# A conditional arm moved behind the ending of a two-layer hybrid kernel, and routing lists built for 60 units in place of 86

## The chip, the cores and the metric

The kernel runs on one core of a Trainium2 chip. The metric is the device time of one execution in microseconds (us). The core has five engines with a queue each: PE (TensorE, with weight loads shown as PEld), DVE (VectorE), ACT (ScalarE), POOL (GpSimd) and SP (SyncE, which here only issues transfers and loads registers). Each engine works through its own instructions in order and waits on semaphores for the others.

## The reference

The input is an image of 256 channels by 64 by 64. Layer 0 is a windowed linear attention and is not touched by the change. Layer 1 works on 4096 tokens of 256 channels: full softmax attention, then a mixture of eight experts of which each token uses two. What matters here is the expert part:

```python
logits = xt @ Wr + br
probs = jax.nn.softmax(logits, axis=-1)
top_p, top_idx = jax.lax.top_k(probs, TOP_K)          # TOP_K = 2 of 8 experts
weights = top_p / top_p.sum(axis=-1, keepdims=True)
...
h = jax.nn.gelu(jnp.einsum('end,edh->enh', xe, W1) + b1[:, None, :], approximate=False)
y = jnp.einsum('enh,ehd->end', h, W2) + b2[:, None, :]
...
out = (weights[:, :, None] * sel).sum(axis=1)         # added to t, then back to channels x pixels
```

## The kernel before

**Slots and units.** The kernel doesn't run every expert on every token. It gathers tokens by expert into units of 128 rows; two units make a slot of 256 rows, and some slots have a third unit of 64 rows. Four early slots (EARLY) are filled from the first tiles while attention still runs. The other 28 usual slots (NS) take 60 units (`USUAL = THIRDS + 2 * NS`). In the worst case the tokens of an input need up to 86 units (NU). Whether the 26 beyond the usual ones are needed is known only at run time.

**Lists.** `route_and_run` ranks the router's logits, counts tokens per expert, and gives every token a place: a unit (`which`) and a row in it (`within`). From these it builds, for each of the 86 units, the list of the token rows to read (`source`) and of the rows to write (`target`). It does this with one-hot matrices in eight steps of eight token tiles. In each step DVE builds `line` (L1690) and two thirds of `piece` (L1693 and L1697), ACT the other third (L1696), and PE adds eight small products into the PSUM tile `back` (L1699, shown as ps_acc). A piece is 8 x NU elements wide per partition. A helper `owners` (L1628 to L1650) works out which expert each slot belongs to, for the usual slots and the 26 later units alike, and the flag `more_slots`. At the end `row_ops` (L972 to L978) turns `back` into `source` and `target`. PE's matmuls for the early slots go on between these products.

**The slots themselves.** `run` is a generator over slots. For each slot SP loads the weights of the expert (L1380; for usual slots it first loads the expert's number into a register, L1360), POOL gathers the rows (L1401, from the DRAM tensor `zrows`), PE transposes them (L1420), PE and ACT compute the hidden layer (L1450 matmul, L1453 gelu), PE the second product (L1467), DVE adds the bias (L1471), and POOL scatters the rows to the DRAM tensor `yrows` (L1472). `zrows` is written by SP (L1525) from rows that ACT scales (L1521) between the gelus of the early slots. The order of all these on each engine is set by a scheduler, which follows the order of the program text but moves instructions by its own estimate of their times.

**The arm and the ending.** All of the attention and of the usual slots stands in the taken side of a branch (`tc.If(tame > 0)`, L1744). Behind it every engine loads the flag `more_slots` into a register (L2028) and branches on it (L2030, `tc.If(more > 0)`). The arm computes units 60 to 85. When it is skipped, each engine jumps over it to a short block that brings the semaphores to the values that the arm would have left, and from there to the ending. In that short block POOL waits for all its scatters and then raises the semaphores of its own transfers (INC_SWDGE_SEM). Then comes the ending: for four bands of the image and two groups of four tiles in each, SP loads the rows of the first expert and ACT those of the second from `yrows` (L2048, 512 KB each, four buffers per set), DVE adds both into the residual `t` with the router's weights `top` (L2052, two instructions a tile), PE transposes (L2058), ACT copies to the image (L2059), and SP and ACT store one band at a time (L2065). The last lines, L2090, are the waits and barriers that end the program.

Of the kernel before, what the change touches and what calls it, by code (L numbers as in the profile page):

```python
# [56 lines left out]
AWAY = 200.0 * P  # L57
TAME = 60.0
# [62 lines left out]
def tile_conv_attn_hybrid(ctx: ExitStack, tc: tile.TileContext, a: dict, out: bass.AP):  # L121
# [100 lines left out]
    def tok(i):  # L222
        return slice(P * i, P * (i + 1))
# [757 lines left out]
    def all_of(ops):  # L981
        for op in ops:
            op()
# [169 lines left out]
    with ExitStack() as phase:  # L1153
# [196 lines left out]
        more_slots = of_last(1, dt=I32)  # L1350

# [134 lines left out]

        def route_and_run(work_on, slot_ps, beside, done):

            with ExitStack() as experts:
# [16 lines left out]
                with ExitStack() as routing:  # L1506
# [73 lines left out]
                    size, ends, begins = (small.tile([P, 2, NE], F32, name=x) for x in ("size", "ends", "begins"))  # L1580
# [15 lines left out]
                    units_used = small.tile([P, 1], F32, name="units_used")  # L1596
# [26 lines left out]
                    def owners():  # L1623

                        n = NU - USUAL
                        slot_of = small.tile([P, NS + n], F32, name="slot_of")
                        late, unit = slot_of[:, NS:], cst["unit"]
                        over = small.tile([P, n], F32, name="over")  # L1628
                        full = small.tile([P, 1], F32, name="full")
                        nc.vector.tensor_copy(slot_of[:, :NS], iota[:, :NS])  # L1630
                        nc.vector.tensor_scalar_add(full, units_used, float(THIRDS))
                        nc.vector.tensor_scalar(over, unit[:, :n], full, None, op0=ALU.is_ge)
                        nc.vector.scalar_tensor_tensor(
                            late, unit[:, 2 * n :], units_used, over, op0=ALU.subtract, op1=ALU.mult
                        )
                        nc.vector.tensor_add(late, late, unit[:, n : 2 * n])
                        past = small.tile([P, NS + n, 2 * NE], F32, name="past")
                        nc.vector.tensor_tensor(
                            past,
                            slot_of.unsqueeze(2).to_broadcast([P, NS + n, 2 * NE]),  # L1640
                            ends.rearrange("p n e -> p (n e)").unsqueeze(1).to_broadcast([P, NS + n, 2 * NE]),
                            ALU.is_ge,
                        )
                        owner = small.tile([P, NS + n], F32, name="owner")
                        nc.vector.tensor_reduce(owner, past, AX.X, ALU.add)
                        nc.vector.tensor_copy(expert_of, owner)
                        nc.vector.tensor_single_scalar(expert_of, expert_of, NE - 1, op=ALU.bitwise_and)
                        nc.vector.tensor_scalar_add(full, with_thirds, float(NS - THIRDS))
                        nc.vector.tensor_tensor(full, full, slots_used, ALU.max)
                        nc.vector.tensor_single_scalar(more_slots, full, float(NS), op=ALU.is_gt)  # L1650
# [22 lines left out]
                    NPC = NU  # L1673
                    G = 8
                    counter = r_work.tile([P, P, G], BF16, name="counter", bufs=1)
                    nc.gpsimd.tensor_copy(counter, iota.unsqueeze(2).to_broadcast([P, P, G]))
                    units = r_work.tile([P, NPC], BF16, name="units", bufs=1)
                    nc.gpsimd.tensor_copy(units, iota[:, :NPC])
                    back = r_ps.tile([P, CH], F32, tag="acc", name="ps_acc", bufs=1)
                    for n in range(2):  # L1680
                        pos = one(f"pos{n}")
                        whole, low = (small.tile([P, NT], I32, name=f"{x}{n}") for x in ("whole", "part"))
                        which, within = (small.tile([P, NT], BF16, name=f"{x}{n}") for x in ("which", "within"))
                        all_of(position_ops(hots[n], row, each(f"at{n}"), pos, whole, low, within, which, 0))
                        high = small.tile([P, NT], BF16, name=f"high{n}")
                        nc.gpsimd.tensor_copy(high, cst["high"][:, NT * n : NT * (n + 1)])
                        for i8 in range(0, NT, G):
                            some = lambda v, n: v[:, i8 : i8 + G].unsqueeze(1).to_broadcast([P, n, G])
                            line = r_work.tile([P, P, G], BF16, name="line")
                            made = nc.vector.tensor_tensor(line, some(within, P), counter, ALU.is_equal)  # L1690
                            piece = r_work.tile([P, 3, G, NPC], BF16, name="piece")
                            on_units = lambda v: v[:, i8 : i8 + G].unsqueeze(2).to_broadcast([P, G, NPC])
                            nc.vector.tensor_tensor(  # L1693
                                piece[:, 0], on_units(which), units.unsqueeze(1).to_broadcast([P, G, NPC]), ALU.is_equal
                            )
                            nc.scalar.activation(piece[:, 1], piece[:, 0], AF.Copy, scale=cst["number"])  # L1696
                            nc.vector.tensor_mul(piece[:, 2], piece[:, 0], on_units(high))  # L1697
                            for i in range(G):
                                nc.tensor.matmul(  # L1699
                                    back[:, : 2 * NPC].rearrange("p (m n) -> p m n", m=2),  # L1700
                                    line[:, :, i],
                                    piece[:, 1:, i, :],
                                    start=n == 0 and i8 + i == 0,
                                    stop=n == 1 and i8 + i == NT - 1,
                                )
                            if n == 0 and i8 == G:
                                with tc.issue_after(made.ins):
                                    owners()
                            advance(1)

                    advance(2)
# [3 lines left out]
                    high = small.tile([P, NPC], F32, name="high")  # L1715
                    nc.vector.tensor_copy(high, back[:, NPC : 2 * NPC])
                    got, second, spare = (small.tile([P, NPC], F32, name=x) for x in ("got", "second", "spare"))
                    all_of(row_ops(source, target, back[:, :NPC], high, got, second, spare, cst["spare"]))
# [309 lines left out]
        more = nc.values_load(more_slots[:1, :1], min_val=0, max_val=1)  # L2028
        with (
            tc.If(more > 0),  # L2030
            psum("m_ps2", 2) as ps,
        ):
            one_bank = lambda: ps.tile([P, KC * SLOT], F32, tag="tp", name="ps_tp")
            for _ in run([(None, q) for q in range(USUAL, NU)], [ps], [], {}, one_bank):
                pass

        with ExitStack() as ending:
            pool = lambda name, bufs: ending.enter_context(tc.tile_pool(name=name, bufs=bufs))
            ps = ending.enter_context(psum("o_ps", 4))
            work = pool("o_work", 4)  # L2040
            img = act.rearrange("p k (y x) -> p k y x", x=IMG)
            by_band = yrows[: 2 * N, :].rearrange("(n i b p) c -> n b p i c", n=2, b=NB, p=P)
            for b in range(NB):
                for i4 in range(0, NCH, 4):
                    ys = []
                    for n in range(2):
                        ys.append(work.tile([P, 4, C], F32, tag=f"y{n}", name=f"y{n}"))
                        (nc.scalar if n else nc.sync).dma_start(ys[n], by_band[n, b, :, i4 : i4 + 4, :])  # L2048
                    for i in range(4):
                        at = NB * (i4 + i) + b  # L2050
                        for n in range(2):
                            nc.vector.scalar_tensor_tensor(  # L2052
                                t[:, at, :C], ys[n][:, i, :], top[n][:, at : at + 1], t[:, at, :C],
                                op0=ALU.mult, op1=ALU.add,
                            )
                        op = ps.tile([P, CH], F32, tag="mm", name="ps_mm")
                        for k in range(KC):
                            nc.tensor.transpose(op[:, tok(k)], t[:, at, tok(k)], ident)  # L2058
# [35 lines left out]
```

## Time and profile before

| | us |
|---|---|
| median of 3 runs | 2750.59 (2749.43 to 2750.81) |
| the profiled execution | 2754.69 |
| its span in the trace | 2752.9 |
| busy PE / DVE / ACT / POOL | 2638.8 / 1880.4 / 1502.6 / 820.5 |
| lists are built (first line to last product) | 2240.0 to 2262.7 |
| last expert matmuls end | about 2704.5 |
| last scatter to `yrows` issued | 2705.24 |
| first load of the ending issued | 2713.44 |
| last store of the ending issued | 2747.7 |

Times inside the execution are microseconds from the start of the span. A row of a group gives a line of the kernel, an engine, an operation and its tile, then how often it ran, its shortest, median and longest time in ns, and when the first and the last of them began. "POOLq", "SPq" and the like are the sequencers of the engines: instructions that only wait, branch, load registers or issue a transfer.

### The profile page before, as it was taken

What the parts mean: (1) busy time and instruction counts of PE and PEld (TensorE: products, weight loads), DVE (VectorE), ACT (ScalarE), POOL (GpSimd) and SP (SyncE); (2) the same over time, 40 slices, a digit from 0 to 9 for tenths busy, and PEclk for the clock granted to TensorE, in tenths of its full rate; (3) what the DMA queues carried; (4) which work ended last, traced back from release to release, by engine and by line L of the source; (5) the groups of instructions that cost most, each with busy time, mean ns of one, the idle gap of its engine ahead of it and who ended that gap; (6) DMA issues with size and microseconds to landing.
All of it is one profiled execution on the core that took longest, in us unless ns stands there. A gap on an engine that the chain in (4) does not pass through costs nothing.

```text
span 2752.9 us, 71916 instructions
## 1 busy us (share of the span) xinstructions
PE 2638.8 (96%) x30978; PEld 1189.6 (43%) x30978; DVE 1880.4 (68%) x2534; ACT 1502.6 (55%) x2079; POOL 820.5 (30%) x919
## 2 busy tenths in 40 slices
PE   6889999997999999999999999999999999999995
PEld 5454336744433556211212121212121278888883
DVE  6758688666878876788888888888888871111114
ACT  3323323222333334899898989898989852222222
POOL 2057777404777752000000010000001123222220
PEclk9999999999999999999999999999999999999996
DMA  5000000000000000455555555555656645555555
GB/s 145 7 23 25 11 28 22 7 13 23 21 15 25 25 22 1 91 118 115 113 113 113 119 112 108 116 116 110 139 107 137 153 147 175 194 187 179 187 174 193
DMA packets 114467, 256.65 MB, mean 93 GB/s; under 512 B 19890, under 2 KB 76440, under 8 KB 100052
## 3 DMA queue, kind: packets, MB, share of 16 engines
q0 software_dynamic: 22240, 132.66, 23.1%
q1 hardware_dynamic: 84724, 110.30, 12.4%
q10 hardware_dynamic: 7168, 8.92, 1.0%
q8 instruction: 247, 4.05, 0.6%
q14 instruction: 88, 0.72, 0.1%
HBM read 118.64 MB, written 17.86 MB: 50 GB/s over the span
## 4 chain that ended last, share of the span: by engine, by line
PE 91%; DVE 3%; DMA 3%; issue 2%; ACT 0%; POOL 0%; ACTq 0%; SPq 0%; DVEq 0%; POOLq 0%
PE ps_three L1799 19%; PE ps_acc L1758 18%; PE ps_sc L826 8%; PE ps_yp L1467 7%; PE ps_hp L1450 7%; PE ps_acc L842 7%; PE ps_sc L726 3%; PE ps_sc L753 3%; PE ps_acc L784 3%; PE ps_two L411 2%; PE ps_mm L1242 2%; PE ps_two L444 2%; DMA yrows<-v,qk 2%; PE ps_two L525 1%; PE ps_acc L772 1%
## 5 line engine op out<-in xcount | busy, mean ns | idle before, releaser
L1799 PE MATMUL ps_three<-qk 32*64 32x512 f32 x6144 | 563.2, 612 | 2.3 <-DVE t L1737 1.3
L1799 PE MATMUL ps_one<-qk 32*64 32x512 f32 x2048 | 556.2, 613 | 0.2 <-ACT pe L1808 0.2
L646 ACT COPY sm<-ps_sc 128x384 f32<-128x384 f32 (+3 forms) x454 | 218.3, 510 | 526.5 <-PE ps_sc L826 339.0
L1831 DVE TENSOR_TENSOR act<-act,pe 128x2048 f32<-128x2048 f32 x195 | 448.1, 2298 | 83.4 <-ACT pe L1811 51.3
L1811 ACT ACTIVATE pe<-ps_three 128x1536 f32<-128x1536 f32 x330 | 477.4, 1447 | 0.0
L653 DVE TENSOR_TENSOR sm<-ps_sc,mask 128x512 f32<-128x512 f32 (+3 forms) x740 | 340.1, 519 | 69.2 <-PE ps_sc L826 66.1
L653 POOL TENSOR_TENSOR sm<-sm,mask 128x192 f32<-128x192 f32 (+3 forms) x428 | 349.5, 846 | 114.3 <-ACT sm L646 114.0
L1831 DVE TENSOR_TENSOR act<-act 128x2048 f32<-128x2048 f32 x150 | 343.8, 2292 | 50.3 <-ACT act L1811 37.1
L1819 POOL DMA_DIRECT2D pe<-pe x108 | 93.0, 861 | 940.1 <-ACT pe L1811 625.1
L1758 PE MATMUL ps_acc<-pe,v 128*32 128x512 f32 x2640 | 351.6, 605 | 0.0
L1453 ACT ACTIVATE v<-ps_hp,qk 128x256 f32<-128x256 f32 (+1 forms) x256 | 122.8, 480 | 342.8 <-PE ps_hp L1450 338.5
L1799 PEld LDWEIGHTS ps_three<-qk 32*64 32x64 f32 x6144 | 112.5, 129 | 414.5 <-ACT pe L1808 243.2
L1811 ACT ACTIVATE act<-ps_three 128x1536 f32<-128x1536 f32 x182 | 263.2, 1446 | 0.0
L1467 PE MATMUL ps_yp<-qk,v 128*128 128x256 f32 (+1 forms) x1088 | 241.7, 380 | 0.0
L1450 PE MATMUL ps_hp<-qk 128*128 128x256 f32 (+1 forms) x1024 | 236.8, 389 | 2.8 <-ACT v L1453 1.7
L826 PE MATMUL ps_sc<-qk 32*64 32x384 f32 (+3 forms) x3584 | 234.6, 458 | 0.1
L1808 ACT ACTIVATE pe<-ps_one 128x512 f32<-128x512 f32 x330 | 197.3, 598 | 59.0 <-PE ps_one L1799 34.5
L653 POOL TENSOR_TENSOR sm<-sm,ycut 128x384 f32<-128x384 f32 (+4 forms) x146 | 147.1, 1028 | 254.1 <-ACT sm L646 253.8
L1467 PEld LDWEIGHTS ps_yp<-qk,v 128*128 128x128 f32 (+1 forms) x1088 | 200.3, 187 | 30.7 <-issue 1.3
L842 PE MATMUL ps_acc<-sm,v 128*32 128x256 f32 (+3 forms) x2688 | 213.2, 419 | 0.1
L1450 PEld LDWEIGHTS ps_hp<-qk 128*128 128x128 f32 x1024 | 180.7, 189 | 52.7 <-ACT v L1453 13.6
L1758 PE MATMUL ps_acc<-act,v 128*32 128x512 f32 x1456 | 193.9, 604 | 0.0
(359 smaller groups left out, 2868.7 us busy)
## 6 DMA issues: line engine op xcount, KB each, us to landing
pe<-pe POOLq DMA_DIRECT2D x108, 1024.0 KB
qk<-in_L_ffn_W SPq DMA_DIRECT2D x64, 1024.0 KB
by<-recs SPq DMA_DIRECT2D x48, 256.0 KB
rows<-in_x SPq DMA_DIRECT2D x16, 256.0 KB
qk<-in_L_ffn_b SPq DMA_DIRECT2D x32, 128.0 KB
y<-yrows SPq DMA_DIRECT2D x8, 512.0 KB
y<-yrows ACTq DMA_DIRECT2D x8, 512.0 KB
rec<-recs SPq DMA_DIRECT2D x60, 64.0 KB
```

Of the source, the lines that this page charges most:

```text
L646: copied = nc.scalar.copy(sm[:, :used], sc[:, :used])
L653: done = engine.tensor_mul(to, of, mk.unsqueeze(1).to_broadcast(list(to.shape)))
L826: nc.tensor.matmul(scs[h][u : u + rows, at : at + n], kT[hs[h], P * i + u : P * i + u + rows], qT[hs[h], CH * ix + CELL * c0 : CH * ix + C ...
L842: nc.tensor.matmul(acc[hs[h], CELL * c0 : CELL * c1], v[:, i, hs[h]], sms[h][:, at : at + n], start=not begun[0], stop=last and at == plac ...
L1450: nc.tensor.matmul(hp[:, :n], w1[:, k, tok(m)], x_now[:, k, :n], start=k == 0, stop=k == KC - 1)
L1453: done["gelu"] = nc.scalar.activation(hid[:, m, :n], hp[:, :n], AF.Gelu, bias=cols[:, m : m + 1]).ins
L1467: product = nc.tensor.matmul(yp[:n], hid[:, m, P * j : P * j + n], w2[:, m, :], start=m == 0, stop=m == NH - 1)
L1758: nc.tensor.matmul(to[D * hd : D * (hd + 1), :], lhsT(hd), rhs(hd), start=start, stop=stop, skip_group_check=True,)
L1799: nc.tensor.matmul(to[CELL * u : CELL * (u + 1), :], qk[hs, 1, g, P * i + CELL * u : P * i + CELL * (u + 1)], qk[hs, 0, g, chunk(qc)], sta ...
L1808: first = nc.scalar.activation(head(pe, 0), one, AF.Exp, scale=C**-0.5)
L1811: nc.scalar.activation(pe[:, CH:], three.rearrange("p h n -> p (h n)"), AF.Exp, scale=C**-0.5).ins
L1831: latest[:] = [nc.vector.tensor_add(total, total, weights_of[r, i]).ins]
```

## The change

Three things are done. First, the ending becomes a function `finish_all` that is called unconditionally straight behind the attention branch; the flag is loaded and tested after it, and the arm, if taken, computes the extra units and then calls `finish_all` once more. So that it can be called twice, the ending no longer adds into `t`: the first instruction of a tile writes into the first loaded buffer and the second into the second loaded buffer, which PE then transposes. Second, the code that builds the lists becomes `lists_of(first, last, ...)`. The usual path calls it for units 0 to 59; a piece is now 8 x 60 elements. The arm calls it again for units 60 to 85. Third, `owners_of` does the owners of one range: 28 slots on the usual path, the 26 later units in the arm. What the arm needs later (`ends`, `units_used`, `which`, `within`) is kept in a part of the old query buffer (`of_last`) instead of a pool that ends with the routing.

```diff
+        ends, units_used = of_last(2, NE), of_last(1)
+        which, within = ([of_last(NT, dt=BF16) for _ in range(2)] for _ in range(2))
...
+        def owners_of(pool, to, slot_of):
...
+        def lists_of(first, last, small, work, ps, places_of, between):
+            n_units = last - first
...
+            units = work.tile([P, n_units], BF16, name="units", bufs=1)
+            nc.gpsimd.tensor_copy(units, cst["iota"][:, first:last])
...
+                    piece = work.tile([P, 3, LINES, n_units], BF16, name="piece")
...
+                        back[:, : 2 * n_units].rearrange("p (m n) -> p m n", m=2),
...
                     def owners():
 
-                        n = NU - USUAL
-                        slot_of = small.tile([P, NS + n], F32, name="slot_of")
-                        late, unit = slot_of[:, NS:], cst["unit"]
-                        over = small.tile([P, n], F32, name="over")
+                        owners_of(small, expert_of[:, :NS], iota[:, :NS])
                         full = small.tile([P, 1], F32, name="full")
-                        nc.vector.tensor_copy(slot_of[:, :NS], iota[:, :NS])
-                        nc.vector.tensor_scalar_add(full, units_used, float(THIRDS))
-                        nc.vector.tensor_scalar(over, unit[:, :n], full, None, op0=ALU.is_ge)
...
+                    finish_lists = lists_of(0, USUAL, small, r_work, r_ps, places_of, between)
...
+        def finish_all():
...
+                            both = t[:, at, :C]
+                            for n in range(2):
+                                nc.vector.scalar_tensor_tensor(
+                                    ys[n][:, i, :], ys[n][:, i, :], top[n][:, at : at + 1], both,
+                                    op0=ALU.mult, op1=ALU.add,
+                                )
+                                both = ys[n][:, i, :]
+                            op = ps.tile([P, CH], F32, tag="mm", name="ps_mm")
+                            for k in range(KC):
+                                nc.tensor.transpose(op[:, tok(k)], both[:, tok(k)], ident)
...
+        finish_all()
+
+
         more = nc.values_load(more_slots[:1, :1], min_val=0, max_val=1)
-        with (
-            tc.If(more > 0),
-            psum("m_ps2", 2) as ps,
-        ):
-            one_bank = lambda: ps.tile([P, KC * SLOT], F32, tag="tp", name="ps_tp")
-            for _ in run([(None, q) for q in range(USUAL, NU)], [ps], [], {}, one_bank):
-                pass
-
-        with ExitStack() as ending:
...
-                        for n in range(2):
-                            nc.vector.scalar_tensor_tensor(
-                                t[:, at, :C], ys[n][:, i, :], top[n][:, at : at + 1], t[:, at, :C],
-                                op0=ALU.mult, op1=ALU.add,
-                            )
...
-                            nc.tensor.transpose(op[:, tok(k)], t[:, at, tok(k)], ident)
...
+        with tc.If(more > 0):
+            with tc.tile_pool(name="l_small", bufs=1) as small, tc.tile_pool(name="l_work", bufs=2) as work:
+                cst.update(constants_of("m", small))
...
+                owners_of(small, expert_of[:, NS:], slot_of)
+                with psum("l_ps", 1) as ps:
+                    lists_of(USUAL, NU, small, work, ps, lambda n: None, lambda *_: None)()
+            with psum("m_ps2", 2) as ps:
+                one_bank = lambda: ps.tile([P, KC * SLOT], F32, tag="tp", name="ps_tp")
+                for _ in run([(None, q) for q in range(USUAL, NU)], [ps], [], {}, one_bank):
+                    pass
+            finish_all()
```

On the usual path the scheduler also orders some instructions differently where the lists are built. PE ran seven hidden-layer matmuls and four transposes between the second and the third group of list products; now it runs two to four hidden-layer matmuls between any two of the first seven groups, and the last group stands earlier in the second product of its slot. On POOL the scatter of that slot's second unit stood behind the gathers of the next slot and now stands between its second gather and its third, which fetches the 64-row unit. On SP fourteen register loads stand ahead of the next `zrows` store where four stood. Outside this stretch and the tail the order on every engine is the same.

## The prediction

> **What bounds the kernel now.** I read the page first: busy time by engine and the chain that ended last. PE carries the span.
>
> ```profile
> PE 2638.8 (96%) x30978; PEld 1189.6 (43%) x30978; DVE 1880.4 (68%) x2534; ACT 1502.6 (55%) x2079; POOL 820.5 (30%) x919
> PE 91%; DVE 3%; DMA 3%; issue 2%; ACT 0%; POOL 0%; ACTq 0%; SPq 0%; DVEq 0%; POOLq 0%
> ```
>
> The change touches two places, so I read each by itself: the stretch that builds the lists, and the tail behind the last expert matmul. The view by windows (stretch, length, then busy us and instructions of PE, PEld, DVE, ACT, POOL) gives both:
>
> ```profile
> 2240.00:2265.00 25.00, 23.43 (x149) 19.71 (x148) 23.42 (x51) 14.47 (x26) 3.80 (x3) 1.00 0.36 103
> 2265.00:2290.00 25.00, 25.00 (x114) 20.02 (x113) 3.19 (x8) 8.01 (x16) 11.09 (x12) 1.00 0.60 194
> 2708.00:2714.00 6.00, 0.00 (x0) 0.00 (x0) 0.00 (x0) 0.00 (x0) 0.00 (x0) 0.50 0.03 9
> ```
>
> While lists are built, DVE is nearly full but PE idles only 25.00 - 23.43 = 1.57 us; then PE is full until about 2704.5. From 2708 to 2714 no engine computes and the DMA share is 0.03: an empty hole. What fills it is told by the tail's branch and wait lines. First POOL's sequencer:
>
> ```profile
> L1744 POOLq COMPARE_BRANCH  x2: 40/40/41, 1105.4 to 2705.0; - x2
> L2028 POOLq EVENT_SEMAPHORE  x1: 43/43/43, 2709.1 to 2709.1; - x1
> L2030 POOLq COMPARE_BRANCH  x1: 55/55/55, 2709.6 to 2709.6; - x1
> L2030 POOLq EVENT_SEMAPHORE  x4: 17/43/43, 2712.2 to 2712.5; - x4
> L2030 POOLq INC_SWDGE_SEM  x1: 792/792/792, 2712.6 to 2712.6; - x1
> ```
>
> It leaves the attention branch at 2705.0 and is at the flag at 2709.1; it branches at 2709.6 and is on the other side at 2712.2; it raises its semaphores until 2712.6 + 0.79 = 2713.4. Now the waits of the two queues that load the ending's first tiles, and SP's list of waits (total, times, longest):
>
> ```profile
> L2048 ACTq EVENT_SEMAPHORE  x9: 38/38/4369, 2708.9 to 2733.0; - x9
> L2048 SPq EVENT_SEMAPHORE  x8: 17/28/4326, 2708.9 to 2731.5; - x8
> SPq L2048 <- DMA yrows<-v,qk: 28.8, 2, 24.4
> ```
>
> SP waits twice. The long wait, 24.4 us, ends at 2708.9: the last scatter has landed (its last packets are seen between 2708.0 and 2708.5). The other is 28.8 - 24.4 = 4.4 us, one instruction of 4326 ns here and of 4369 ns on ACT, and ends when POOL's increment does. The first load goes out at 2713.44. So 4.4 us pass between data being there and being asked for, and the jump over the arm is what they wait for.
>
> [...] POOL's branch takes 55 ns, the next instruction stands 2.6 us later, and instruction packets move between 2709 and 2710 and between 2712.5 and 2713.5. [...] rows here have 50 to 63 ns apart from PE's 4279 ns, so the fetch, not the branch, is the price. [...]
>
> **The change part by part.** *The arm goes behind the ending.* Built order: the first loads on SP and ACT now wait for the last scatter alone, no longer for POOL's increment. Both queues are there in time: SP left the attention branch at 2677.2, ACT was at the flag at 2700.3. The loads start at 2708.9 + 0.1 in place of 2713.44: **-4.4 us**. DVE (at the flag at 2708.9) and PE (2704.1) need their first tile only about 5 us after that. Behind the loads the ending keeps its pace if nothing else changes: 64 DVE instructions of 0.40 us (25.7 us), with waits of 0.47, 0.63 and 1.59 us for loads. Of the two instructions per tile none is added. The buffer of the second expert's rows is now read by PE too, so ACT asks for its next tile one copy later in three of four turns, about 0.8 us each; a load has 4 to 11 us before it is used, so I take 0, with 2.4 us as the worst. ACT also loses a table load of 1.28 us ahead of its first copy, which only shortens that delay; I take 0 for it.
>
> *What the branch costs at the end.* Every engine now loads the flag, branches, fetches and waits after its last work. Counted back from the shifted end:
>
> ```profile
> L2065 SPq DMA_DIRECT2D out<-act x4: 332/350/351, 2727.1 to 2747.7; - x4
> L2090 SPq DRAIN  x3: 7/7/13, 2751.9 to 2752.3; - x3
> L2030 PEldq COMPARE_BRANCH  x1: 4279/4279/4279, 2704.6 to 2704.6; - x1
> ```
>
> The last stores are issued at 2747.7 and have landed at 2751.9, so there are 4.2 us of cover. ACT: 0.37 to issue, 0.4 for flag and branch, 2.6 to fetch (2700.8 to 2703.4 before) = 3.4 us. SP: 0.35 + 2.4. PE is through at 2746.6 and needs 0.4 + 4.3: 2751.3. All end before 2751.9, PE by 0.6 us only. Left over is what SP does behind the landing, some more waits of 17 to 28 ns and one more jump: **+0.3 us**. Bounds: 0 if nothing shows, and 4.4 if the fetches queue behind the stores (DMA share about a half from 2749 to 2751) so that the whole jump comes back.
>
> *Lists for 60 units.* A piece becomes 480 elements: 866 - 208/0.96 = 649 ns. DVE makes 16 of them and saves 16 x 0.217 = 3.5 us; ACT 8, at most 1.7. `owners` loses five instructions of 0.14 to 0.25 us and halves two of 1.05: about 2 us. Lists are ready some 5 us sooner. But PE can only win its idle 1.57 us, and of its products at most 8 groups x 0.77 us x 52/172 columns = 1.9 us, if they go by width (a group's weight loads take 0.81 us, which stays, so likely none). By hand along the new order, DVE needs 1.8 us for a step, PE's two hidden-layer matmuls and a group of products 1.6 us, and owners comes in between: PE still waits about 1 us. I take 0.6 us gained there, 0 to 2 as bounds.
>
> That gain meets the next slot's gathers:
>
> ```profile
> 2266.37 0.99 POOL L1401 DMA_INDIRECT qk<-zrows,qk  x1 [3.01 <-DVE v L1471]
> 2268.93 0.92 POOL L1401 DMA_INDIRECT v<-zrows,qk  x1 [0.31 <-issue]
> 2272.99 0.33 PE L1420 MATMUL ps_tp<-cst,v 64*128 64x64 f32 x2
> ```
>
> The first gather starts 2.3 us after the lists (2264.06): what it waits for is the last `zrows` store, issued at 2258.80 behind a weight load. Faster lists move that store by half a us at most, since ACT's last scaled rows come behind its last piece. And the third gather now stands behind a scatter, one issue of 1.27 us later. It went out at 2268.93 and PE used it at 2272.99 without waiting; at 3.7 us to land (the last scatter: 2705.24 to 2708.9) it came at about 2272.6. Now: 2268.93 + 1.27 - 0.5 + 3.7 = 2273.4, and PE, due at 2272.4, waits. Net **+0.2 us** (-1.5 to +1).
>
> SP's ten register loads moved ahead of a `zrows` store (about 0.55 us each) begin 4 us sooner and hide beside PE's hidden layer; the weights they precede are used 20 us later.
>
> Sum: -4.4 + 0.3 + 0.2 = -3.9 us. The profiled execution has 2754.69 us, 1.8 outside its span, and becomes 2750.8. It stood 4.1 above the median of the runs, so the median goes from 2750.59 to **2746.7 us**.
>
> **Rivals.** *The lists pay too* (0.25): the third gather lands in time and PE keeps its 1.5 us: -4.4 + 0.3 - 1.3 = -5.4, 2745.2 us. For it: DVE was full; against: the gather's lack of slack. *The jump comes back at the end* (0.15): fetches slowed by stores, PE's first; 2 to 4.4 us returned, about 2749.5 us. For it: PE has 0.6 us of cover; against: the other engines have 0.8 and more. *The change doesn't do what it says* (0.03): if the scatter landed only at 2713.3, loads can't start sooner: 2751.1 us; its packets at 2708 and the two separate waits speak against it. *Slower* (0.05): the loads of the ending. ACT issues them between its copies, in order, and copies behind a late one wait as well. If the four turns ran 2.5 us late each, +10 - 3.9 = +6, 2756.7 us; it decides once a turn is later than the queue of loads in flight, about 4 us. The trace has these loads in flight up to 11.6 us (2728.33 to 2739.97), which speaks against it. The likeliest case keeps 0.52.
>
> **How the numbers follow.** A measurement of this kernel tells about 0.2%, 5.5 us. The likeliest case lies inside, at -3.9. Faster by more takes 2745.1: a bit over half of the first rival and a tenth of the likeliest case, 0.2. Slower by more is the last rival, 0.05. Same: 0.75. The range runs from 2743.8 (gains of 2 us in the lists and none lost at the end, with 0.3 of noise) to 2749.8 (the jump back).
>
> **What would show it.** Right: first loads of the ending about 0.1 us after the last scatter has landed, with no second wait of 4.3 us; lines of the flag after the last stores, PE's branch the last to return; the page's span near 2749; a PE wait of about a us for the 64-row transposes. Wrong: a hole before the loads still there; sequencers still fetching when the stores have landed; longer waits of DVE for loads than 0.47, 0.63 and 1.59 us.

## The result, and the profile after

The changed kernel takes **2755.33 us** (median of 14 runs, 2752.96 to 2760.39) beside 2750.36 us for the kernel before (14 runs, 2748.39 to 2754.35): a ratio of 1.0019, 95% interval 1.0011 to 1.0027, some 5 us slower. The prediction said 2746.7 us, 3.9 us faster. The profiled execution of the changed kernel has 2754.41 us (span 2752.6) and stands 0.9 below its median; that of before stood 4.3 above its own. So the two spans, nearly equal, must not be compared whole. They are compared by stages below.

The page by itself shows nothing: PE's busy time has grown by 1 us.

```profile
PE 2639.9 (96%) x30978; PEld 1190.4 (43%) x30978; DVE 1876.0 (68%) x2529; ACT 1500.3 (55%) x2078; POOL 819.7 (30%) x919
```

The view by windows, for the first two stretches that the prediction shows and two finer ones (stretch, length, busy us and instructions of PE, PEld, DVE, ACT, POOL, then PE's granted clock, DMA share and GB/s):

```profile
2240.00:2265.00 25.00, 23.93 (x150) 20.25 (x150) 14.61 (x38) 14.06 (x30) 2.94 (x3) 1.00 0.46 144
2265.00:2290.00 25.00, 18.62 (x74) 14.12 (x73) 2.44 (x6) 4.56 (x9) 9.63 (x10) 0.86 0.47 151
...
2267.00:2274.00 7.00, 0.95 (x5) 0.51 (x6) 1.00 (x2) 0.17 (x1) 5.24 (x6) 0.73 0.82 267
2274.00:2283.00 9.00, 9.00 (x36) 7.59 (x37) 1.19 (x4) 0.00 (x0) 1.92 (x2) 0.83 0.43 139
```

Where PE was full (25.00 of 25.00 us) it now works 18.62 us at a mean granted clock of 0.86 (1.00 is full speed). In 7 us from 2267 it works 0.95, while the DMA share is 0.82; in the 9 us after, PE is busy throughout, but at a clock of 0.83. The timeline of that place (start, duration, engine, line, operation; in brackets the idle time before and what ended it), lines of several engines:

```profile
2267.00 0.41 PE L1423 MATMUL ps_tp<-cst,qk 128*128 128x128 f32 x2 [0.34 <-DMA qk<-zrows,qk]
...
2267.80 0.93 POOL L1404 DMA_INDIRECT v<-zrows,qk  x1 [0.30 <-issue]
2267.80 1.00 SPq L1383 DMA_DIRECT2D qk<-in_L_ffn_W  x2
...
2268.00 0.44 PE L1423 MATMUL ps_tp<-cst,qk 128*128 128x128 f32 x2 [0.59 <-DMA qk<-zrows,qk]
...
2273.89 0.44 PE L1423 MATMUL ps_tp<-cst,v 64*128 64x64 f32 x2 [5.46 <-DMA v<-zrows,qk]
```

The third gather (64 rows into `v`) and the two weight transfers of the slot after (1 MB each) are issued in the same instant. PE has the rows 6.1 us later. In the kernel before, the same weights go out 10 us behind the third gather (2268.93):

```profile
2279.34 1.43 SPq L1380 DMA_DIRECT2D qk<-in_L_ffn_W  x2
```

There, 15 of SP's register loads stand between the last transfer of the first usual slot's weights (its bias) and those of the second; in the changed order nine do. Both executions can be counted from the matmul that counts the tokens chosen for each expert (`chosen`, at 2228.6 and 2224.2). From there, the second slot's W1 goes out after 50.7 us before and after 43.6 us now. Six loads at 0.56 us are 3.4 us of these 7; 1.6 us come from a start that is sooner by that much (the bias goes out after 37.6 and 36.0 us), and the rest, on balance, from SP instructions that ran slower in the kernel before.

At the end of the kernel the first step of the prediction is seen as it was told: no second wait of 4.3 us ahead of the loads. The lines of the ending's loads, and SP's list of waits:

```profile
L2056 ACTq EVENT_SEMAPHORE  x9: 38/38/38, 2710.2 to 2729.9; - x9
L2056 SPq EVENT_SEMAPHORE  x7: 28/28/26372, 2683.8 to 2727.5; - x7
SPq L2056 <- DMA yrows<-v,qk: 26.4, 1, 26.4
```

The branch on the flag now stands behind everything (durations in ns, then first and last start):

```profile
L2084 SPq EVENT_SEMAPHORE  x9: 17/17/17, 2750.3 to 2750.9; - x9
...
L2084 PEldq COMPARE_BRANCH  x1: 3487/3487/3487, 2743.7 to 2743.7; - x1
L2084 SPq COMPARE_BRANCH  x1: 50/50/50, 2744.7 to 2744.7; - x1
L2084 ACTq COMPARE_BRANCH  x1: 64/64/64, 2745.5 to 2745.5; - x1
...
L2084 PEldq EVENT_SEMAPHORE  x1: 51/51/51, 2747.3 to 2747.3; - x1
L2084 ACTq EVENT_SEMAPHORE  x1: 17/17/17, 2751.7 to 2751.7; - x1
```

SP branches at 2744.7 and is on the other side at 2750.3 (5.6 us); ACT takes from 2745.5 to 2751.7 (6.2 us). The last stores went out at 2744.3, and the last of their packets is seen between 2749.4 and 2749.6. So some 2 us of ACT's jump come after the stores have landed.

All executions can be laid side by side when each is cut at the same instructions. The kernels in the table are those of the experiments below. Layer 0 and the attention before the cut are unchanged code, and their end scatters by up to 9 us between executions; it is left out. Stages: *lists*, from the first matmul on `chosen` to the first hidden-layer matmul of the last early slot; *gathers*, from there to the first hidden-layer matmul of the first usual slot; *slots*, to the last scatter's issue; *tail*, from there to the end. "Sum" is against before; the last column is the measured ratio minus one, times 2750 us, with its interval. A row is one execution, and the end of the span is read to 0.1 us; for "rows first" the sum lies just outside the measured interval.

| kernel | lists | gathers | slots | tail | sum | measured |
|---|---|---|---|---|---|---|
| before | 36.94 | 14.71 | 424.98 | 47.66 | | |
| after | 35.37 | 23.03 | 424.99 | 44.99 | +4.1 | +5.2 (3.0 to 7.4) |
| ending first | 37.04 | 14.71 | 424.98 | 45.31 | -2.2 | -1.1 (-3.6 to 1.1) |
| lists only | 35.38 | 24.89 | 424.96 | 48.40 | +9.3 | +9.9 (6.3 to 13.8) |
| scatter later | 35.37 | 16.95 | 425.53 | 45.08 | -1.4 | +0.3 (-1.9 to 2.8) |
| weights held | 35.41 | 20.61 | 424.98 | 45.14 | +1.8 | +2.5 (0.6 to 4.7) |
| no arm | 35.34 | 25.00 | 424.98 | 41.71 | +2.7 | +2.5 (0.6 to 4.1) |
| loads behind | 35.36 | 15.20 | 424.97 | 45.59 | -3.2 | -2.2 (-4.4 to 0.3) |
| rows first | 35.37 | 14.72 | 424.97 | 45.02 | -4.2 | -2.2 (-4.1 to -0.6) |

The change gains 1.6 us in the lists and 2.7 in the tail, and loses 8.3 at the gathers. The loss is known less well than the gains: "after", "lists only" and "no arm" have the same code up to the end of that stage and spend 23.0, 24.9 and 25.0 us in it.

### The profile page after: what moved, and what is told of

It is laid out like the page before. It is cut to its first block, busy times and chain, and to the rows that moved or that the text cites. A ratio compares the mean times of both kernels' runs of the same rounds, so it can differ in the third digit from the quotient of the medians.

```text
span 2752.6 us, 71914 instructions
## 1 busy us (share of the span) xinstructions
PE 2639.9 (96%) x30978; PEld 1190.4 (43%) x30978; DVE 1876.0 (68%) x2529; ACT 1500.3 (55%) x2078; POOL 819.7 (30%) x919
```

## The experiments

**Each half alone.** First the moved arm: the kernel before, with

```diff
-        more = nc.values_load(...)      # arm, then the ending
-        with (tc.If(more > 0), psum("m_ps2", 2) as ps): ...
-        with ExitStack() as ending: ...
+        finish_all()
+        more = nc.values_load(...)
+        with tc.If(more > 0):
+            ...                         # the arm of before, lists of 86 units
+            finish_all()
```

> The kernel before with one part of the change alone: the arm stands behind the ending, which it redoes; the lists keep all 86 units and the arm builds none. Theory A (the change loses at the gathers of the first usual slot and gains about 2.7 us in the tail): 2750.4 - 2.7 = about 2747.7 us, no PE wait of more than 1 us for the 64-row gather, and from the last stores' issue to the end about 8.3 us instead of 5.2. Rival B (the ending, its buffers or the branch at the end lose more than the removed jump gave): 2753 to 2756 us, with the last scatter at the same time as before.

Measured: ratio 0.9996 (0.9987 to 1.0004). By runs alone a gain can't be told from none; the stages of one execution show it: 14.71 us at the gathers as before and 2.35 off the tail (the first load 2.75 us behind the last scatter instead of 8.20; the last stores' issue to the end 7.86 instead of 5.20). Rival B's 2753 to 2756 us is out. Then the lists alone, the changed kernel with

```diff
-        finish_all()
         more = nc.values_load(...)
         with tc.If(more > 0):
             ...
-            finish_all()
+        finish_all()
```

> The changed kernel with the arm put back ahead of the ending, which then runs once: the lists of 60 units alone are left of the change. Theory A: the lists stage gains 1.5 us and the gathers behind it cost 6.4 us of PE waits and about 1.4 us of a lower PE clock, so 2755.3 + 2.7 = about 2758 us, the slowest of these runs, with a PE wait of 5 to 6 us for the 64-row gather. Rival B (the tail is at fault): 2749 to 2750.5 us.

Measured: 1.0036 (1.0023 to 1.0050), the slowest of all: +9.9 us, where some 7.6 were expected, inside the interval.

```profile
2278.01 0.45 PE L1423 MATMUL ps_tp<-cst,v 64*128 64x64 f32 x2 [5.56 <-DMA v<-zrows,qk]
2278.39 10.11 PE L1470 MATMUL ps_yp<-qk,v 128*128 128x256 f32 x32
```

The wait for the 64-row gather is 5.56 us, and PE is slower behind it: 10.11 us for 32 products that take 7.17 in the kernel before. The loss belongs to the lists, the gain to the arm.

**What makes the third gather late.** On POOL it stands behind a scatter; on SP the next weights come early. One experiment turns each. First the scatter, kept until the gathers are issued:

```diff
+                if kept:
+                    with tc.issue_after(done["gather"]):
+                        scatter(*kept.pop())
...
+                    if slot[0] == EARLY - 2 and j == 1:
+                        kept.append((to[:n, q : q + 1], y))
+                    else:
+                        scatter(to[:n, q : q + 1], y)
```

> The changed kernel with POOL's order turned at one place: the second scatter of the early slot is issued behind the three gathers of the first usual slot, not between the second and the third. Theory C (the third gather is late because it stands behind that scatter): it is issued 1.27 us earlier, ahead of the next slot's weights, and lands in about 3.3 us, so PE's wait falls from 5.5 to about 1.4 us: about 2750.5 us. Theory D (it lands late because the next slot's 2 MB of weights are in flight from 2267.8): still 6 us to land, the wait only falls to 4.2 us: about 2754 us. Theory E (all three gathers are late, because the last zrows store went out late behind SP's register loads and W1): the waits of 0.34 and 0.59 us for the first two gathers stay whatever is done here.

Measured: 1.0001 (0.9993 to 1.0010), and from its timelines (the third gather, which now goes out ahead of the scatter; PE's three waits and the products; then the weights on SP; last, a window):

```profile
2267.27 0.92 POOL L1404 DMA_INDIRECT v<-zrows,qk  x1 [0.30 <-issue]
...
2267.61 0.41 PE L1423 MATMUL ps_tp<-cst,qk 128*128 128x128 f32 x2 [0.30 <-DMA qk<-zrows,qk]
2268.92 0.44 PE L1423 MATMUL ps_tp<-cst,qk 128*128 128x128 f32 x2 [0.90 <-DMA qk<-zrows,qk]
2269.95 0.30 PE L1423 MATMUL ps_tp<-cst,v 64*128 64x64 f32 x2 [0.59 <-DMA v<-zrows,qk]
2270.18 7.17 PE L1483 MATMUL ps_yp<-qk,v 128*128 128x256 f32 x32
```

```profile
2268.44 1.00 SPq L1383 DMA_DIRECT2D qk<-in_L_ffn_W  x2
```

```profile
2270.00:2280.00 10.00, 9.71 (x43) 7.83 (x44) 1.75 (x5) 0.78 (x2) 5.58 (x6) 1.00 0.83 288
```

The gather goes out 1.2 us ahead of the weights and needs 2.7 us, and PE waits 0.59 us for it instead of 5.46. The products run at full pace (7.17 us, clock 1.00), although the weights are in flight beside them (DMA share 0.83). The waits for the first two gathers stay (0.30 and 0.90 us), as theory E said. Now the other side, the weights held and the scatter kept ahead:

```diff
+                if slot in usual and usual.index(slot) == EARLY + 1:
+                    after = nc.sync.dma_start(mark, done["entered"][:1, 0, :1]).ins
+                with tc.issue_after(after) if after else nullcontext():
...
+                        with tc.issue_after(done["scatter"]) if first_third else nullcontext():
```

> The changed kernel with the weights of the second usual slot held on SP until the rows of the first usual slot are transposed (a 4-byte transfer that waits for them stands ahead of those weights), POOL's order kept with the scatter ahead of the third gather. Theory D (the weights in flight slow the third gather): it lands 3.7 us after its issue at 2267.8, PE waits about 3.1 us instead of 5.5: about 2752.5 us. Theory C (the place behind the scatter alone): no change, 2755.3 us, the wait 5.5 us. Theory E: the waits of 0.34 and 0.59 us for the first two gathers stay.

Measured: 1.0009 (1.0002 to 1.0017). The second slot's weights go out at 2275.58. POOL's and PE's lines:

```profile
2270.96 0.93 POOL L1410 DMA_INDIRECT v<-zrows,qk  x1 [0.30 <-issue]
```

```profile
2273.70 0.44 PE L1429 MATMUL ps_tp<-cst,v 64*128 64x64 f32 x2 [2.14 <-DMA v<-zrows,qk]
2274.07 8.57 PE L1477 MATMUL ps_yp<-qk,v 128*128 128x256 f32 x32
```

Behind the scatter, but without weights in flight, the gather again needs 2.7 us. So both theories hold, and each cause needs the other: the scatter moves the gather's issue back by 1.3 us, into the weights, and **the weights turn 2.7 us into 6**. Holding the weights doesn't make the kernel as fast as before, though: the waits for all three gathers, 3.90 us in sum, stay. In four executions the weights were issued at the same time as the gather or up to 2.6 us ahead of it; they have 6.1, 6.4, 6.8 and 6.1 us from issue to PE's use (after, lists only, no arm, and the first of the two memset kernels below). In three the gather was issued ahead of the weights or long after them; they have 2.7, 2.7 and 2.6 (scatter later, weights held, and the second memset kernel). How 64 small rows share the DMA engines with 2 MB is not shown; the traces show the effect, 2.7 us against 6.

**Why all three gathers are late.** In the kernel before, the last `zrows` store goes out 1.0 us after the last scaled row is written (2257.83 to 2258.80). In the changed one it is 2.8 us (2253.24 to 2256.03). SP's lines, of before and then of after:

```profile
2258.32 0.38 SPq L1380 DMA_DIRECT2D qk<-in_L_ffn_W  x1
2258.80 0.41 SPq L1525 DMA_DIRECT2D zrows<-act  x1
...
2254.12 0.37 SPq L1373 DMA_DIRECT2D qk<-crows  x1
2254.73 1.19 SPq L1383 DMA_DIRECT2D qk<-in_L_ffn_W  x1
2256.03 0.41 SPq L1592 DMA_DIRECT2D zrows<-act  x1
```

In the changed kernel SP has 19 register loads to do from 2241.3 on, 14 of them ahead of the last store but one and five between that and the last, where `crows` and W1 stand too. W1's issue also takes 1.19 us instead of 0.38; why is not shown. The next kernel is the changed one with the later slots' register loads behind the first usual slot's weights:

```diff
-                e = nc.values_load(expert_of[:1, s : s + 1], ...)
+                with tc.issue_after(done["usual"]) if "usual" in done else nullcontext():
+                    e = nc.values_load(expert_of[:1, s : s + 1], ...)
...
+            if early is None:
+                done.setdefault("usual", came.ins)
```

> The changed kernel with one order turned on SP: the register loads for the second and later usual slots are issued behind the weights of the first usual slot, so that only one of them is left ahead of the last zrows store. Theory E (all gathers are late because that store is late): it goes out within half a us of the last scaled row, the gathers start some 3 us sooner in the stage, PE waits for none of them, the stage from the hidden layer of the last early slot to that of the first usual slot falls from 23.0 to 14.7 us, and the sum of the stages lies 4 us under the kernel before: 2746 to 2748 us. Rival (the gathers wait on something else, such as their buffers or POOL): the stage stays at 17 us or more as with the scatter moved, about 2752 us.

```profile
2253.15 0.38 SPq L1384 DMA_DIRECT2D qk<-in_L_ffn_W  x1
2253.64 0.41 SPq L1595 DMA_DIRECT2D zrows<-act  x1
```

```profile
2266.84 0.60 PE L1426 MATMUL ps_tp<-cst,qk 128*128 128x128 f32 x4
2267.89 0.30 PE L1426 MATMUL ps_tp<-cst,v 64*128 64x64 f32 x2 [0.45 <-PE ps_tp L1426]
```

The store goes out 0.05 us after its rows (2253.59). The next slot's weights, behind 13 register loads again, go out at 2273.3. The scheduler's order on POOL came out different too: the third gather now stands ahead of the scatter. The first two gathers are waited for no longer. The view puts the 0.45 us ahead of the 64 rows down to PE, but they fit a gather issued at 2265.25 and 2.6 us on its way. The stage is 15.2 us, and the ratio 0.9992 (0.9984 to 1.0001). Last, the weights behind the store too:

```diff
+                if slot[0] is None and "usual" not in done:
+                    after = done.get("stored")      # the last zrows store
```

> As the run before (register loads behind the first usual slot's weights), and those weights themselves stand behind the last zrows store, so that no weights share the DMA with it. Theory E: the store lands in about 3 us instead of 8, the gathers start as soon as the lists are there, no PE wait for gathers: 14.7 us for the stage, 2746 to 2748 us, no better than the run before since the gathers were off the path there already. Rival (weights come late instead): a PE wait of 1 us or more for the first usual slot's W1 or W2, and 2749 us or more.

```profile
2268.30 0.60 PE L1428 MATMUL ps_tp<-cst,qk 128*128 128x128 f32 x4
2268.83 0.33 PE L1428 MATMUL ps_tp<-cst,v 64*128 64x64 f32 x2
2269.09 7.17 PE L1475 MATMUL ps_yp<-qk,v 128*128 128x256 f32 x32
```

No wait, 14.72 us as in the kernel before (14.71), and a ratio of **0.9992 (0.9985 to 0.9998)**: this version is some 2 us faster than the kernel before, and so faster than the changed one. The store still took 5.4 us until the first gather (2255.08 to 2260.52), not the 3 expected; W1 and W2 went out behind it, at 2257.20 and 2257.82, while it was on its way. That it is no better than the run before was expected. So turning SP's order gives back the loss at the gathers, all but 0.5 us of it in the first of the two kernels and all of it in the second. POOL's order moved as well in both, but in the second the scatter still stands ahead of the third gather (2261.81 and 2264.40), so its place is not what cures that one.

**What the branch costs at the end.** The changed kernel without arm, flag and branch:

```diff
         finish_all()
-        more = nc.values_load(...)
-        with tc.If(more > 0): ...
```

> The changed kernel without the arm, its flag's load and the branch (the units beyond the usual slots, none of which is used with these inputs, are left out). Everything up to the last stores is as in the changed kernel. If the branch and its instruction fetch hold up the end: from the last stores' issue to the end about 5.2 us instead of 8.3, so 2755.3 - 3.1 = about 2752.2 us. If the stores' own landing sets the end, as the prediction had it (0.3 us given back): about 2755 us.

From the last stores' issue to the end it is 5.21 us instead of 8.28. The branch costs 3.1 us there. The other kernels agree: 5.1 to 5.2 us where no branch stands behind the stores (before, lists only), 7.9 to 8.5 where one does. The ratio is 1.0009 (1.0002 to 1.0015); that interval overlaps the changed kernel's, so the 3.1 us rest on the traces and not on the runs.

The last three experiments ran once each, and only their traces are read. Is it the stores in flight that slow the fetch of the instructions behind the branch? In the changed kernel one instruction packet starts between 2744.6 and 2745.7, none from 2745.8 to 2747.8, where the stores' packets take a DMA share of 0.94, and five from 2747.8 to 2749.0. That a jump's time goes into this fetch is a reading of such packets; measured are the times of the jumps. The version with the rows first, without the last band's two stores:

```diff
-                    for k in range(KC):
+                    for k in range(KC if b < stored else 0):
```

> The kernel with the rows stored first, without the two stores of the ending's last band (an eighth of the output each is left out), so that nothing is in flight when the flag is tested. If the stores in flight slow the instruction fetch at the end: SP's jump takes 2.4 to 2.9 us as it did for POOL in the kernel before, instead of 5.6, and the other engines are across at about 3 us behind the last copy, so the span ends about 4 us behind the last copy. If the fetch is as slow by itself: SP and ACT are across 5.6 to 6.2 us behind the last copy, as in the changed kernel.

```profile
L2089 SPq COMPARE_BRANCH  x1: 50/50/50, 2728.8 to 2728.8; - x1
...
L2089 ACTq COMPARE_BRANCH  x1: 59/59/59, 2736.5 to 2736.5; - x1
...
L2089 ACTq EVENT_SEMAPHORE  x1: 17/17/17, 2739.3 to 2739.3; - x1
```

ACT is across in 2.9 us instead of 6.0 (2739.0 to 2745.0 in the same version with them), and the span ends at 2740.8, 4.4 us behind the last copy (2736.4) instead of 8.2. SP branched earlier here, 0.4 us behind the issue of the two stores of the band before (2728.43), and still took 5.5 us (2728.8 to 2734.3), against the 2.4 to 2.9 expected. ACT's branch came 8.1 us behind these two; in the kernel before, the last two had landed after 4.2. There SP's jump took 2.5 us at a DMA share of 0.01. Two jumps at the same time are not the reason: in the kernel before, DVE and POOL branch 0.16 us apart and take 2.8 and 2.7 us. So the stores in flight are what slows ACT. For SP that fits, but no run leaves its transfers out.

**Whether idle time or the weights make PE slower behind the wait.** The version with the rows first, memsets on POOL ahead of the third gather:

```diff
+                            with tc.issue_after(came):
+                                for _ in range(20):          # 40 in the second
+                                    came = nc.gpsimd.memset(idle, 0.0).ins
```

> The kernel with the rows stored first, where 20 small memsets on POOL (about 0.2 us each) and the scatter stand ahead of the third gather and the later gathers behind it; no weights move. The third gather goes out some 5 us later and PE idles about 3.6 us there. If idle time by itself lowers the PE clock afterwards, the next 32 products take 8 us or more instead of 7.17 and the stage is 14.7 + 3.6 + 1.5 = about 20 us; if the slower products of the changed kernel came from the weights in flight, they take 7.2 us and the stage is 18.3 us.

> As the run before with 40 memsets: PE idles some 8 us (up to 11 if the next weights catch up with the gather). If idle time lowers the clock: 3 us or more of slower products behind it, more than with 20; if not, 7.2 us for the next 32 products.

The weights did move, against what was expected: with 20 memsets (0.26 us each, 11 in 2.85) they went out at 2266.4, ahead of the gather, and PE idled 9.42 us; with 40 it idled 7.85, with 10 of the 32 products ahead of the wait. For the question this is no harm. The windows of the first:

```profile
2270.00:2275.00 5.00, 0.00 (x0) 0.00 (x0) 0.00 (x0) 0.00 (x0) 3.82 (x4) 0.50 1.03 339
2275.00:2280.00 5.00, 4.87 (x16) 4.06 (x17) 0.59 (x2) 0.00 (x0) 0.96 (x2) 0.67 0.15 48
```

While PE idles its granted clock is 0.50; in the 5 us after the wait it is 0.67, with the DMA share at 0.15. Little is in flight any more, and PE is slow all the same: 8.56 us for the 32 products. With 40 memsets the slower products cost 2.9 us, about the 3 expected. The other half of the question is answered above: with the scatter moved, 2 MB of weights were in flight beside the products and these took 7.17 us at a clock of 1.00. It is the idle time.

## Why the prediction was wrong

- *"The first loads go out without POOL's increment: -4.4 us."* Right. From the landing of the last scatter to the first load 0.2 us pass instead of 4.6, which is the 4.4 us foretold, and the ending's own pace is kept (33.96 us from first load to last store, 34.26 before). Another 1.1 us was not foretold and is luck: the last scatter landed 2.55 us after its issue instead of 3.62, so that the first load comes 2.75 us behind that issue instead of 8.20. It is alike in every run with the branch behind the ending or without one (2.4 to 2.6 us); why is not shown. The slower rival, late loads of the ending, did not come.
- *"+0.3 us at the end, PE the last to return."* **Failed in size**: 3.1 us. The cover of 4.2 us was right where no branch follows (from the last stores' issue to the end 5.21 us without the arm, 5.20 before), but SP and ACT were given 2.4 and 2.6 us for the fetch, times from jumps with the DMA nearly idle (share 0.01 and 0.08). Behind their own stores they took 5.6 and 6.2. The prediction also read the DMA share from 2749 to 2751 as about a half. That is the share of one of the two stores' queues (0.54 and 0.49); both together fill it (1.03). PE, thought to be the tightest, was across at 2747.3. This was the second rival, with the wrong engine. The tail nets -2.7 where -4.1 was told, the luck above included.
- *"0.6 us gained in the lists."* 1.6 us, inside its bounds. A piece takes 650 ns, as worked out (649): 208 elements fewer took 216 ns less, the 0.96 elements a ns of that estimate. In the kernel before, DVE instructions of 864 and 256 elements (`past` and `row`) took 1048 and 424 ns, 0.97 elements a ns. Unlike what was thought likely, a group of eight products takes 0.65 us instead of 0.77.
- *"SP's register loads hide; the weights they precede are used 20 us later."* **This step failed, and it decided the sign.** It asked when those weights are used, not what they do when they are issued. The loads had been a fence: with 15 of them behind the first usual slot's weights, the next 2 MB kept clear of the gathers. With six fewer there, the weights came 7 us sooner. Those now in front held the last rows back, 2.8 us behind their making instead of 1.0. The prediction had that store up to half a us sooner; counted from the matmul on `chosen`, it went out 1.6 us later (31.8 us instead of 30.2). Both effects count: with the weights held alone the kernel is still 2.5 us slower than before, and with SP's order turned it is 2.2 us faster.
- *"3.7 us to land ... +0.2 us."* **Failed in size**: of the 8.3 us more in this stage, 6.4 are PE waits and 1.9 a slower PE, which the prediction did not have at all. The 3.7 us were those of one scatter with no weights in flight; the gather needed 6.1 with them. By the prediction's own numbers the step is +0.4 and not +0.2 (2273.4 against 2272.99), which changes little. That the third gather would be the one PE waits for most was right; the range for it ended at +1.

Sum of the stages: -1.6 + 8.3 - 2.7 = +4.0 us (+4.1 with all digits), and 5 in the runs.

## What to carry to other kernels

Cheap instructions in front of a transfer also set its time (six register loads of 0.56 us fewer, and the weights came 7 us sooner): when a change lets a queue run ahead, ask which transfers now start sooner and whose small, urgent transfer they meet. A landing time, or the time of a jump, is only good for the traffic under which it was read: here a gather's 2.7 us became 6.1 beside weights, and ACT's 2.9 us across the branch became 6.0 behind stores. And when a stage gets faster, first look at what was ordered behind it: here the faster lists pay only once the rows' store stands ahead of the register loads and weights.

## What the runs showed of the hardware

- A long wait of PE cost more than its length. What lies above 14.71 us and the waits themselves in the stage of the gathers is the price. It is 1.9 us after 6.39 us of waits (after), 3.1 after 7.16 (no arm), 3.5 after 6.66 (lists only), 1.6 after 9.42 and 2.9 after 7.85 (memsets).
- The granted clock fell during such a wait and came back late. In the changed kernel it still read 1.00 from 2269.2 to 2270.2, where PE idled, then 0.50 from 2270.2 to 2277.0, 2.7 us into the products, and 1.00 behind that. With 20 memsets it was 0.50 in the last 5 us of the wait and 0.67 in the 5 us behind it. The costs don't follow the length of the wait; why is not shown.
- Short waits added up. With the weights held, three waits of 1.13, 0.63 and 2.14 us with only transposes between them cost 2.0 us as well. From the last hidden-layer matmul to the first product 5.1 us passed, and the mean clock from 2270 to 2280 was 0.83. With the scatter moved, that stretch was 2.9 us with waits of 1.79 us in sum, and the mean clock was 1.00 from 2260 to 2270 and from 2270 to 2280. Whether transposes count as work for the clock is not shown.
- ACT's jump took 2.6 us in the kernel before, with a DMA share of 0.08, and 2.9 us without the last band's stores. Behind two stores of 512 KB on two queues it took 6.2 us in the changed kernel and 6.0 in the version with the rows first.
